# Routed results of a second MoE layer: written tile by tile and gathered, or scattered to a row per token and expert and loaded plainly

## The chip, the cores and the metric

The kernel runs on one core of one Trainium2 chip. The core has TensorE (PE; its weight loads are listed apart as PEld), VectorE (DVE), ScalarE (ACT), GpSimd (POOL) and SyncE (SP), each with an instruction queue of its own, and 16 DMA engines. In this kernel SP issues the plain DMAs and POOL the indirect ones. The metric is the device time in microseconds of one execution, the median of several runs.

## The reference

Two transformer blocks over 8 sequences of 512 tokens with 256 features, float32. Block 0: causal attention with rotary positions, then a mixture of 32 experts (top 8, inner size 96). Block 1: causal attention with a fused projection, then a mixture of 16 experts (top 2, inner size 176) and a shared expert (inner size 352). The change sits in the last of these:

```python
scores = softmax(t @ gate_w.T)
weights, indices = top_k(scores, 2)            # 2 of 16 experts for each token
for e in range(16):
    w_e = sum(where(indices == e, weights, 0))
    y = y + swiglu(t, w1[e], w3[e], w2[e]) * w_e[:, None]
z = swiglu(t, sw1, sw3, sw2)                   # shared expert
return x + y + z
```

with swiglu(t, a, b, o) = (silu(t a') * (t b')) o'. Each token therefore has two routed results, which are added to its row of x.

## The kernel before

**Routing.** The routed layers don't multiply every token with every expert. While a layer's attention runs, `route` works out for each token and each of its chosen experts a row in a DRAM buffer `xg`, in which every expert has a slab, and POOL scatters the token's normalized row there with indirect DMAs of 128 rows (L385). Behind a row's 256 features stand its weights for the layer's experts, so in layer 1 an `xg` row has 272 floats. The rows behind each slab's last token, up to the next full tile, are overwritten with zeros. `tables` then finds, for a list of tiles of 128 rows, where each begins (`rowi`) and which expert it belongs to (`offi`); the list has a fixed length, so some of its tiles hold few or no tokens.

**Parts.** Layer 1 is split: part 0 holds sequences 0 to 5 (60 tiles), part 1 sequences 6 and 7 (28 tiles).

**Experts.** `experts` goes over the tiles in 44 pairs, in five stages that are spread over the steps s of one loop: `load` of pair s (SP loads two tiles of `xg`, 7 buffers), `turn_x` of pair s-4 (PE transposes, DVE copies to `xgTs`, L1108), `gate_up` of pair s-5 (PE, L1131; ACT silu, L1136; DVE multiplies with the other half and with the row's weight, which it takes from the `xg` row at an offset in a register, L1123), `turn_h` of pair s-6 (PE transposes, DVE copies to `hTs`, L1152) and `down` of pair s-7 (PE `y`, L1162; ACT copies it to `ys`, L1167; SP writes the 256 KB of a pair to consecutive rows of `yg`, L1168). PE's order is the order in which this loop is written; the order of the other engines' instructions is chosen by the scheduler.

**Results.** When part 0 is through, `results` runs beside part 1's pairs. For each sequence, `begin` fetches x back, and `gather_rows` works out which rows of `yg` hold each token's two results (L1186 to L1192 on DVE: two tensor operations, four MAX8, one conversion); POOL gathers them in 8 indirect DMAs of 128 rows into two tiles `g` (L1262). DVE adds both to x (L1274), PE transposes x (`xout`, L1284), ACT copies it (L1285) and SP writes the output (L1286). `begin` of the next sequence is issued before the adds of the current one. `Beside.step` spreads these steps evenly over the loop: 8 steps for each sequence from `done`, the 38th step, to `end`. Sequences 6 and 7 come after the loop, from the second call of `results` in `last_part`, and nothing runs beside them.

A second, general version of the whole computation stands behind a branch (L1516) for inputs that the fast version can't treat; it is not executed with these inputs.

Of the kernel before, what the change touches and what calls it, by code (L numbers as in the profile page):

```python
# [90 lines left out]
def two_blocks_kernel(  # L91
# [117 lines left out]
    class Layer:  # L209
        def __init__(self, n, part, seqs, n_e, k, gu):  # L210
            self.n, self.part, self.seqs, self.n_e, self.k, self.gu = n, part, seqs, n_e, k, gu
            self.name = f"{n}{part}"
            self.w_r = rw[:, : ND * E0] if n == 0 else rw[:, ND * E0 :]

            self.cap = len(seqs) * T + P


            self.most_tiles = len(seqs) * T * k // P + n_e
            self.n_tiles = len(seqs) * T * k // P + n_e // 2 + (6 if n_e > 16 else 4)
            name = self.name  # L220

            self.width = D + n_e
            self.xg = drp.tile([n_e * self.cap + P, self.width], F32, tag=f"xg{name}", name=f"xg{name}")
            self.yg = drp.tile([self.most_tiles * P, D], F32, tag=f"yg{name}", name=f"yg{name}")

            self.slab = cpool.tile([P, n_e], F32, tag=f"slab{name}", name=f"slab{name}")
            nc.gpsimd.iota(
                self.slab, [[self.cap, n_e]], base=1, channel_multiplier=0, allow_small_or_imprecise_dtypes=True
            )
            self.next = cpool.tile([P, n_e], F32, tag=f"next{name}", name=f"next{name}")  # L230
            nc.vector.tensor_copy(self.next, self.slab)
            self.shift = cpool.tile([P, n_e], F32, tag=f"shift{name}", name=f"shift{name}")

            def routes(what, width, dtype):
                return {
                    b: rpool.tile([P, NT, width], dtype, tag=f"{what}{n}", name=f"{what}{n}_{b}") for b in seqs
                }

            self.keys, self.chosen = routes("key", n_e, F32), routes("chosen", n_e, BF16)
# [73 lines left out]
    def ffn_parts(smp, bank):  # L313
        def route(n, b, xn, xT, name, again):
# [65 lines left out]
                nc.vector.max(out=keys[:, t, :], in_=key[:, t, :])  # L380
            rows = rpool.tile([P, NT, k], U32, tag=f"rows{n}", name=f"rows_{name}", bufs=4)
            nc.vector.tensor_scalar(rows, keys[:, :, :k], -1.0, 0.0, ALU.add, ALU.max)  # L382
            for t in range(NT):
                for i in range(k):
                    inst = nc.gpsimd.indirect_dma_start(  # L385
                        out=lay.xg, out_offset=bass.IndirectOffsetOnAxis(ap=rows[:, t, i : i + 1], axis=0),
                        in_=xn[:, t, :], in_offset=None,
                    )
                    tc.declare_no_dep(inst.ins, group=group, reason="no two tokens have the same row")
                    tc.add_to_no_dep_group(group, inst.ins)  # L390
# [671 lines left out]
    def experts(n, gu, dn, mp, ps, again, beside):  # L1062
# [48 lines left out]
        def gate_up(lay, i):  # L1111
            part = lay.part
            xT, xg = made.pop(("xT", part, i)), made.pop(("xg", part, i))
            h = mp.tile([P, 2, inner], F32, tag="h", name=f"h_{name}_{part}_{i}")
            if n == 0:
                whole = ps.tile([P, 2, 2 * inner], F32, tag="gu", name=f"gu_{name}_{part}_{i}")
                gus = [whole[:, 0, :], whole[:, 1, :]]
            else:
                gus = [ps.tile([P, 2 * inner], F32, tag="gu", name=f"gu_{name}_{part}_{i + j}") for j in range(2)]

            def scaled(j):

                nc.vector.scalar_tensor_tensor(  # L1123
                    h[:, j, :], h[:, j, :], xg[:, j, D:][:, bass.ds(offs[part, i + j][2], 1)], gus[j][:, inner:],
                    ALU.mult, ALU.mult,
                )

            for j in range(2):
                at = offs[part, i + j][0]
                for c in range(ND):  # L1130
                    nc.tensor.matmul(  # L1131
                        gus[j], xT[:, j, c, :], gu[:, bass.ds(at + c * 2 * inner, 2 * inner)],
                        start=(c == 0), stop=(c == ND - 1),
                    )
                if n:
                    nc.scalar.activation(h[:, j, :], gus[j][:, :inner], AF.Silu)  # L1136
                    scaled(j)
            if n == 0:
                nc.scalar.activation(h, whole[:, :, :inner], AF.Silu)  # L1139
                for j in range(2):  # L1140
                    scaled(j)
            made["h", part, i] = h
# [12 lines left out]
        def down(lay, i):  # L1155
            part = lay.part
            hT = made.pop(("hT", part, i))
            y = ps.tile([P, 2, D], F32, tag="y", name=f"y_{name}_{part}_{i}")
            for j in range(2):
                at = offs[part, i + j][1]  # L1160
                for q, (lo, n_in) in enumerate(chunks):
                    nc.tensor.matmul(  # L1162
                        y[:, j, :], hT[:n_in, q, j, :], dn[:n_in, bass.ds(at + q * D, D)],
                        start=(q == 0), stop=(q == n_ch - 1),
                    )
            ys = mp.tile([P, 2, D], F32, tag="ys", name=f"ys_{name}_{part}_{i}", bufs=4)
            nc.scalar.copy(ys, y)  # L1167
            nc.sync.dma_start(out=lay.yg[i * P : (i + 2) * P, :].rearrange("(j p) d -> p j d", p=P), in_=ys)  # L1168

# [6 lines left out]
                beside.step(s)  # L1178
            beside.finish()

    def gather_rows(n, b, gat, again=""):

        lay = lay_of(n, b)
        n_e, k, name = lay.n_e, lay.k, f"{n}{again}_{b}"
        key = gat.tile([P, NT, n_e], F32, tag="ykey", name=f"ykey{name}", bufs=1)
        nc.vector.tensor_tensor(key, lay.keys[b], lay.shift.unsqueeze(1).to_broadcast([P, NT, n_e]), ALU.add)  # L1186
        nc.vector.tensor_tensor(key, key, lay.chosen[b], ALU.mult)
        keys = gat.tile([P, NT, 8], F32, tag="ykeys", name=f"ykeys{name}", bufs=2)
        for t in range(NT):
            nc.vector.max(out=keys[:, t, :], in_=key[:, t, :])  # L1190
        rows = rpool.tile([P, NT, k], U32, tag=f"yrows{n}", name=f"yrows{name}")
        nc.vector.tensor_scalar(rows, keys[:, :, :k], -1.0, lay.tiles(bool(again)) * P - 1.0, ALU.add, ALU.min)  # L1192
        for i in range(k):
            for t in range(NT):
                yield i, t, lay.yg[: lay.tiles(bool(again)) * P, :], bass.IndirectOffsetOnAxis(ap=rows[:, t, i : i + 1], axis=0)

    def gathers(n, b, gat, again=""):

        for i, t, yg, rows in gather_rows(n, b, gat, again):
            nc.gpsimd.indirect_dma_start(  # L1200
                out=xs[b][:, t, :], out_offset=None, in_=yg, in_offset=rows, compute_op=ALU.add
            )
            if t % 2:
                yield

    def load_attn(pool, src, cols, width, layer):
        t = pool.tile([P, width], F32, tag="attn_w", name=f"attn_w{layer}")
# [47 lines left out]
    def results(seqs, gat, op, ps, again="", behind=lambda: None):  # L1255


        def begin(b):
            fetch_x(b, x_after[1], f"c1{again}")
            made[b] = [gat.tile([P, NT, D], F32, tag="gath", name=f"g1{again}_{b}_{i}", bufs=2 * K1) for i in range(K1)]  # L1260
            for i, t, yg, rows in gather_rows(1, b, gat, again):
                nc.gpsimd.indirect_dma_start(out=made[b][i][:, t, :], out_offset=None, in_=yg, in_offset=rows)  # L1262
                if t % 2:
                    yield

        made = {}
        yield from begin(seqs[0])
# [54 lines left out]
    def all_experts(n, gw, gat, again=False, weights=()):  # L1322
# [6 lines left out]
        with ExitStack() as s:  # L1329
# [11 lines left out]
            def x_in_ring():  # L1341
                for b in range(SPLIT[0]):
                    fetch_x(b, x_after[0], f"a1{g}")
                yield
                for b in range(SPLIT[0]):
                    yield from gathers(0, b, gat, g)

            def x_kept():
                with tc.issue_after(beside.load):
# [19 lines left out]
            if n == 0:  # L1369
                beside.add(done, end, SPLIT[0] * 16 + 1, x_in_ring())  # L1370
            else:
                beside.add(
                    done, end, SPLIT[1] * 8, results(range(SPLIT[1]), gat, gat, ps, g, lambda: beside.last)
                )
            experts(n, gw, dw, mp, ps, again, beside)
            return beside.last
# [28 lines left out]
    with ExitStack() as s1:  # L1405
# [4 lines left out]
        with ExitStack() as s:  # L1410
# [7 lines left out]
            def ahead1(b):  # L1418
                if b >= SPLIT[0]:
# [1 line left out]
                    with tc.issue_after(fetched):  # L1421
                        load_gate_up(gw1, f1, I1, N1R, b - SPLIT[0], NB - SPLIT[0])
                    yield
                    yield from gathers(0, b, gat)

            def after1(b):
                name = f"f1_{b}"
                xn = layernorm(xs[b], lnp, name, "xn_rows", 1, E1)
                yield from free()
                xT = yield from turned(xn, lnp, bank, name)  # L1430
                yield from route(1, b, xn, xT, name, False)
# [43 lines left out]
    def general1(gat):  # L1475
        with ExitStack() as s:
# [20 lines left out]
            def all_of(b, name):  # L1497
                if b >= SPLIT[0]:
                    fetch_x(b, x_after[0], "a1g")
                    drain(gathers(0, b, gat, "g"))  # L1500
                yield from attention1(b, w)
                xn = layernorm(xs[b], lnp, name, "xn_rows", 1, E1)
                xT = yield from turned(xn, lnp, bank, name)
                yield from route(1, b, xn, xT, name, True)
                yield from shared(sw1, xT, xs[b], name)
# [179 lines left out]
```

## Time and profile before

| | us |
|---|---|
| median of 3 runs | 1705.48 |
| lowest, highest | 1697.82, 1710.20 |
| profiled execution | 1701.29 |
| its span in the trace | 1699.6 |
| first gate-and-up product of layer 1's experts | 1428.71 |
| first gather of part 0's results | 1590.09 |
| last y of the experts ends | 1663.48 |
| last add to x begins | 1688.68 |

The profile is one execution; the span is what the trace covers of it, and the mean granted TensorE clock in it was 0.961 of full speed. Durations of single instructions come from that execution. In a list of instructions, "[0.30 <-issue]" gives the idle time of the engine before the instruction and what ended it. In a table of stretches, each engine has its busy time and, in brackets, its number of instructions.

### The profile page before, as it was taken

The numbers are of one execution on the slowest core, as the hardware profiler recorded it, in microseconds if no ns is written. First come the engines' busy times: TensorE is split into PE (matmuls) and PEld (weight loads), VectorE is DVE, ScalarE is ACT, GpSimd is POOL, SyncE is SP. The second block draws the span as 40 slices with busy tenths as digits, with TensorE's granted clock in tenths as the row PEclk, the third lists the DMA queues.
The fourth block names the chain that finished last, engine by engine and source line by source line (L and its number), as shares of the span: only waits on it lengthen the run. The fifth ranks groups of instructions, "written<-read, shape, count | busy, mean of one in ns | idle before, by whom it ended". The sixth has DMA issues, their size and how long they took to land. (4 is left out here: it accounts for less than half of the span.)

```text
span 1699.6 us, 30922 instructions
## 1 busy us (share of the span) xinstructions
PE 1543.7 (91%) x10180; PEld 1029.0 (61%) x10180; DVE 992.0 (58%) x3131; ACT 650.7 (38%) x865; POOL 792.1 (47%) x660
## 2 busy tenths in 40 slices
PE   5899999995999999999989999999899988999982
PEld 2455454543898999998853454544444545777761
DVE  5678887875555555555455764764656544444452
ACT  2555554552233333333334554454355331222221
POOL 0017677577710004888888448888511011000473
PEclk9999999997999999999999999999899998999996
DMA  2035557236988778999995245664312024343563
GB/s 73 13 87 156 163 167 270 102 139 207 307 256 269 202 201 226 266 264 273 268 194 71 39 107 80 127 136 72 86 52 79 26 84 159 109 159 116 156 225 120
DMA packets 255128, 259.43 MB, mean 153 GB/s; under 512 B 80212, under 2 KB 235988, under 8 KB 254964
## 3 DMA queue, kind: packets, MB, share of 16 engines
q1 hardware_dynamic: 199172, 167.88, 32.5%
q0 software_dynamic: 55296, 88.65, 23.0%
q8 instruction: 87, 1.43, 0.4%
q10 hardware_dynamic: 496, 0.85, 0.1%
q14 instruction: 77, 0.63, 0.1%
HBM read 132.70 MB, written 124.57 MB: 151 GB/s over the span
## 5 line engine op out<-in xcount | busy, mean ns | idle before, releaser
L1200 POOL DMA_INDIRECT x_a<-yg,yrows x256 | 402.9, 1574 | 277.2 <-DMA xg_m<-xg 181.9
L385 POOL DMA_INDIRECT xg<-xn_f,rows_f x320 | 321.2, 1004 | 414.7 <-DVE rows_f L382 197.3
L643 ACT ACTIVATE p_a<-st_a 128x2048 f32<-128x2048 f32 (+1 forms) x192 | 306.1, 1594 | 276.4 <-PE st_a L638 243.2
L1131 PE MATMUL gu_m<-gw,xgTs_m 128*128 x1552 | 335.6, 360 | 4.9 <-DVE xgTs_m L1108 3.0
L1131 PEld LDWEIGHTS gu_m<-gw,xgTs_m 128*128 128x128 f32 x1552 | 258.1, 192 | 33.9 <-DVE xgTs_m L1108 3.2
L1162 PE MATMUL y_m<-dw,hTs_m 96*128 (+1 forms) x952 | 237.7, 379 | 0.0
L638 PE MATMUL st_a<-qT_a,kT_a 32*128 32x512 f32 (+3 forms) x2048 | 202.1, 478 | 11.1 <-ACT p_a L643 10.8
L649 DVE TENSOR_TENSOR p_a<-p_a,causal 128x512 f32<-128x512 f32 x256 | 170.8, 686 | 57.3 <-ACT p_a L643 56.1
L661 PE MATMUL o_a<-p_a,v 128*32 128x512 f32 (+3 forms) x2048 | 197.4, 455 | 6.9 <-DVE p_a L649 6.7
L1108 DVE COPY xgTs_m<-xgT_m 128x512 f32<-128x512 f32 x194 | 133.9, 690 | 109.7 <-PE xgT_m L1106 109.4
L1167 ACT COPY ys_m<-y_m 128x512 f32<-128x512 f32 x194 | 113.7, 586 | 189.1 <-PE y_m L1162 174.7
L1123 DVE SCALAR_TENSOR_TENSOR h_m<-h_m,xg_m,gu_m 128x96 f32<-128x96 f32 (+1 forms) x388 | 114.8, 326 | 115.2 <-ACT h_m L1136 69.3
L1162 PEld LDWEIGHTS y_m<-dw,hTs_m 96*128 96x128 f32 (+1 forms) x952 | 165.3, 190 | 15.1
L1262 POOL DMA_INDIRECT g<-yg,yrows x64 | 65.2, 1018 | 202.2 <-DVE h_m L1123 170.9
L638 PEld LDWEIGHTS st_a<-qT_a,kT_a 32*128 32x128 f32 x2048 | 90.1, 189 | 107.2 <-issue 52.4
L1152 DVE COPY hTs_m<-hT_m 96x256 f32<-96x256 f32 (+1 forms) x194 | 92.7, 478 | 99.5 <-PE hT_m L1151 98.5
L1106 PE MATMUL xgT_m<-ident,xg_m 128*128 128x128 f32 x776 | 119.3, 275 | 16.0 <-DMA xg_m<-xg 13.2
L1139 ACT ACTIVATE h_m<-gu_m 128x192 f32<-128x192 f32 x150 | 49.7, 331 | 212.2 <-PE gu_m L1131 200.6
L1106 PEld LDWEIGHTS xgT_m<-ident,xg_m 128*128 128x128 f32 x776 | 95.6, 141 | 39.2 <-issue 16.6
L661 PEld LDWEIGHTS o_a<-p_a,v 128*32 128x32 f32 x2048 | 49.3, 110 | 107.8 <-issue 66.1
L1151 PE MATMUL hT_m<-ident,h_m 128*96 128x128 f32 (+1 forms) x476 | 84.9, 274 | 0.6 <-DVE h_m L1123 0.4
L667 DVE COPY osb_a<-o_a 128x512 f32<-128x512 f32 x64 | 44.0, 688 | 53.0 <-PE o_a L661 53.0
(198 smaller groups left out, 1689.6 us busy)
## 6 DMA issues: line engine op xcount, KB each, us to landing
yg<-ys_m SPq DMA_DIRECT2D x194, 256.0 KB
xg_m<-xg SPq DMA_DIRECT2D x300, 144.0 KB
xg_m<-xg SPq DMA_DIRECT2D x88, 136.0 KB
xg<-zeros SPq DMA_DIRECT2D x66, 144.0 KB
xg<-xn_f,rows_f POOLq DMA_INDIRECT x320
xg<-zeros SPq DMA_DIRECT2D x34, 136.0 KB
xf<-in_x_dram SPq DMA_DIRECT2D x8, 512.0 KB
x_after<-x_in SPq DMA_DIRECT2D x8, 512.0 KB
```

Source lines behind the costliest of these rows:

```text
L385: inst = nc.gpsimd.indirect_dma_start(out=lay.xg, out_offset=bass.IndirectOffsetOnAxis(ap=rows[:, t, i : i + 1], axis=0), in_=xn[:, t, :], ...
L638: nc.tensor.matmul(st[:, g, at : at + T - j * P], kT[r, j * P : (j + 1) * P], qT[r, j * P :], start=True, stop=True,)
L643: nc.scalar.activation(pt, st[:, :, :width], AF.Exp, scale=SCALE)
L649: self.masked = nc.vector.tensor_tensor(d, d, causal.unsqueeze(1).to_broadcast([P, NG, P]), ALU.mult).ins
L661: nc.tensor.matmul(o[32 * g : 32 * g + 32, j * P :], v1[:, j, v_at + g * (DH + 1) :][:, :32], probs[n][:, g, at : at + T - j * P], start=( ...
L1106: nc.tensor.transpose(tr[:, j, c, :], xg[:, j, c * P : (c + 1) * P], ident)
L1108: nc.vector.tensor_copy(xT, tr)
L1123: nc.vector.scalar_tensor_tensor(h[:, j, :], h[:, j, :], xg[:, j, D:][:, bass.ds(offs[part, i + j][2], 1)], gus[j][:, inner:], ALU.mult, A ...
L1131: nc.tensor.matmul(gus[j], xT[:, j, c, :], gu[:, bass.ds(at + c * 2 * inner, 2 * inner)], start=(c == 0), stop=(c == ND - 1),)
L1162: nc.tensor.matmul(y[:, j, :], hT[:n_in, q, j, :], dn[:n_in, bass.ds(at + q * D, D)], start=(q == 0), stop=(q == n_ch - 1),)
L1167: nc.scalar.copy(ys, y)
L1200: nc.gpsimd.indirect_dma_start(out=xs[b][:, t, :], out_offset=None, in_=yg, in_offset=rows, compute_op=ALU.add)
```

## The change

In layer 1 each routed row also carries where its result belongs. Layer 0 keeps its way.

- An `xg` row of layer 1 has 288 floats instead of 272: behind the 16 weights stand 16 integers. For a token that an expert was chosen for, the integer is the number of the token's result row plus one: the token's place in the part for its expert with the higher row, and the same plus the number of the part's tokens for the other. `route` writes them with two more DVE operations for each sequence; the token numbers come from an iota on POOL at the start. Rows of zeros carry 0.
- `gate_up` takes, for each of a pair's two tiles, the integer of the tile's expert minus one into a column of `to` (one DVE operation of 128x1 each; the tile has 5 buffers).
- `down` doesn't write `ys` with SP. POOL scatters it with two indirect DMAs of 128 rows of 1 KB, at the row numbers in `to`; a number out of bounds (the -1 of empty rows) is skipped.
- `yg` of layer 1 is thus ordered by token. `begin` loads a sequence's two tiles `g` with two plain DMAs of 512 KB on SP; the work of `gather_rows` and the gathers are gone from layer 1, and `gather_rows` is merged into layer 0's `gathers`.
- `results` beside part 1 begins two steps later and has 6 steps for each sequence.

```diff
-            self.width = D + n_e
+            self.width = D + n_e * (1 + n)
...
+                self.yg = drp.tile([k * len(seqs) * T, D], F32, tag=f"yg{name}", name=f"yg{name}")
+                self.tokens = cpool.tile([P, len(seqs), NT], F32, tag=f"tokens{name}", name=f"tokens{name}")
+                nc.gpsimd.iota(
+                    self.tokens, [[T, len(seqs)], [1, NT]], base=1, channel_multiplier=NT,
+                    allow_small_or_imprecise_dtypes=True,
+                )
...
             nc.vector.tensor_scalar(rows, keys[:, :, :k], -1.0, 0.0, ALU.add, ALU.max)
+            if n:
+                nc.vector.tensor_tensor(key, key, keys[:, :, 0:1].to_broadcast([P, NT, n_e]), ALU.is_lt)
+                tokens = lay.tokens[:, b - lay.seqs[0], :].unsqueeze(2).to_broadcast([P, NT, n_e])
+                nc.vector.scalar_tensor_tensor(
+                    xn[:, :, D + n_e :].bitcast(I32), key, float(len(lay.seqs) * T), tokens, ALU.mult, ALU.add
+                )
...
             h = mp.tile([P, 2, inner], F32, tag="h", name=f"h_{name}_{part}_{i}")
+            if n:
+                to = made["to", part, i] = mp.tile([P, 2], I32, tag="to", name=f"to_{name}_{part}_{i}", bufs=5)
+                for j in range(2):
+                    nc.vector.tensor_scalar(
+                        to[:, j : j + 1], xg.bitcast(I32)[:, j, D + lay.n_e :][:, bass.ds(offs[part, i + j][2], 1)],
+                        -1.0, None, ALU.add,
+                    )
...
             nc.scalar.copy(ys, y)
-            nc.sync.dma_start(out=lay.yg[i * P : (i + 2) * P, :].rearrange("(j p) d -> p j d", p=P), in_=ys)
+            if n == 0:
+                nc.sync.dma_start(out=lay.yg[i * P : (i + 2) * P, :].rearrange("(j p) d -> p j d", p=P), in_=ys)
+                return
+            to = made.pop(("to", part, i))
+            for j in range(2):
+                inst = nc.gpsimd.indirect_dma_start(
+                    out=lay.yg, out_offset=bass.IndirectOffsetOnAxis(ap=to.bitcast(U32)[:, j : j + 1], axis=0),
+                    in_=ys[:, j, :], in_offset=None, bounds_check=lay.k * len(lay.seqs) * T - 1, oob_is_err=False,
+                )
...
             made[b] = [gat.tile([P, NT, D], F32, tag="gath", name=f"g1{again}_{b}_{i}", bufs=2 * K1) for i in range(K1)]
-            for i, t, yg, rows in gather_rows(1, b, gat, again):
-                nc.gpsimd.indirect_dma_start(out=made[b][i][:, t, :], out_offset=None, in_=yg, in_offset=rows)
-                if t % 2:
-                    yield
+            for i in range(K1):
+                lo = (i * len(lay.seqs) + b - lay.seqs[0]) * T
+                nc.sync.dma_start(out=made[b][i], in_=lay.yg[lo : lo + T, :].rearrange("(p t) d -> p t d", t=NT))
+                yield
...
-                    done, end, SPLIT[1] * 8, results(range(SPLIT[1]), gat, gat, ps, g, lambda: beside.last)
+                    done + 2, end, SPLIT[1] * 6, results(range(SPLIT[1]), gat, gat, ps, g, lambda: beside.last)
...
-                xn = layernorm(xs[b], lnp, name, "xn_rows", 1, E1)
+                xn = layernorm(xs[b], lnp, name, "xn_rows", 1, 2 * E1)
```

More of the change, by code (lines that the diff above doesn't have):

```diff
@@ L220, in __init__ @@
             name = self.name
-            self.width = D + n_e
+            self.width = D + n_e * (1 + n)
             self.xg = drp.tile([n_e * self.cap + P, self.width], F32, tag=f"xg{name}", name=f"xg{name}")
-            self.yg = drp.tile([self.most_tiles * P, D], F32, tag=f"yg{name}", name=f"yg{name}")
+            if n == 0:
+                self.yg = drp.tile([self.most_tiles * P, D], F32, tag=f"yg{name}", name=f"yg{name}")
+            else:
+                self.yg = drp.tile([k * len(seqs) * T, D], F32, tag=f"yg{name}", name=f"yg{name}")
[4 more added lines that the diff above has]
+                )
             self.slab = cpool.tile([P, n_e], F32, tag=f"slab{name}", name=f"slab{name}")
@@ L1167, in down @@
             nc.scalar.copy(ys, y)
-            nc.sync.dma_start(out=lay.yg[i * P : (i + 2) * P, :].rearrange("(j p) d -> p j d", p=P), in_=ys)
+            if n == 0:
+                nc.sync.dma_start(out=lay.yg[i * P : (i + 2) * P, :].rearrange("(j p) d -> p j d", p=P), in_=ys)
[6 more added lines that the diff above has]
+                )
+                tc.declare_no_dep(inst.ins, group=f"to_{name}_{part}", reason="each token's row is one expert's")
+                tc.add_to_no_dep_group(f"to_{name}_{part}", inst.ins)
         stages = [(load, 0), (turn_x, 4), (gate_up, 5), (turn_h, 6), (down, 7)]
@@ L1179, in experts, with gathers @@
             beside.finish()
-    def gather_rows(n, b, gat, again=""):
-        lay = lay_of(n, b)
-        n_e, k, name = lay.n_e, lay.k, f"{n}{again}_{b}"
+    def gathers(b, gat, again=""):
+        lay = lay_of(0, b)
+        n_e, k, name = lay.n_e, lay.k, f"{again}_{b}"
         key = gat.tile([P, NT, n_e], F32, tag="ykey", name=f"ykey{name}", bufs=1)
@@ L1190, in gather_rows @@
             nc.vector.max(out=keys[:, t, :], in_=key[:, t, :])
-        rows = rpool.tile([P, NT, k], U32, tag=f"yrows{n}", name=f"yrows{name}")
+        rows = rpool.tile([P, NT, k], U32, tag="yrows", name=f"yrows{name}")
         nc.vector.tensor_scalar(rows, keys[:, :, :k], -1.0, lay.tiles(bool(again)) * P - 1.0, ALU.add, ALU.min)
@@ L1194, in gather_rows @@
             for t in range(NT):
[L1195 to L1202, printed above, removed]
-            if t % 2:
-                yield
+                nc.gpsimd.indirect_dma_start(
+                    out=xs[b][:, t, :], out_offset=None, in_=lay.yg[: lay.tiles(bool(again)) * P, :],
+                    in_offset=bass.IndirectOffsetOnAxis(ap=rows[:, t, i : i + 1], axis=0), compute_op=ALU.add,
+                )
+                if t % 2:
+                    yield
     def load_attn(pool, src, cols, width, layer):
@@ L1259, in begin @@
             fetch_x(b, x_after[1], f"c1{again}")
+            lay = lay_of(1, b)
             made[b] = [gat.tile([P, NT, D], F32, tag="gath", name=f"g1{again}_{b}_{i}", bufs=2 * K1) for i in range(K1)]
-            for i, t, yg, rows in gather_rows(1, b, gat, again):
-                nc.gpsimd.indirect_dma_start(out=made[b][i][:, t, :], out_offset=None, in_=yg, in_offset=rows)
-                if t % 2:
-                    yield
+            for i in range(K1):
+                lo = (i * len(lay.seqs) + b - lay.seqs[0]) * T
+                nc.sync.dma_start(out=made[b][i], in_=lay.yg[lo : lo + T, :].rearrange("(p t) d -> p t d", t=NT))
+                yield
         made = {}
@@ L1345, in x_in_ring @@
                 for b in range(SPLIT[0]):
-                    yield from gathers(0, b, gat, g)
+                    yield from gathers(b, gat, g)
             def x_kept():
@@ L1423, in ahead1 @@
                     yield
-                    yield from gathers(0, b, gat)
+                    yield from gathers(b, gat)
             def after1(b):
                 name = f"f1_{b}"
-                xn = layernorm(xs[b], lnp, name, "xn_rows", 1, E1)
+                xn = layernorm(xs[b], lnp, name, "xn_rows", 1, 2 * E1)
                 yield from free()
@@ L1499, in all_of @@
                     fetch_x(b, x_after[0], "a1g")
-                    drain(gathers(0, b, gat, "g"))
+                    drain(gathers(b, gat, "g"))
                 yield from attention1(b, w)
-                xn = layernorm(xs[b], lnp, name, "xn_rows", 1, E1)
+                xn = layernorm(xs[b], lnp, name, "xn_rows", 1, 2 * E1)
                 xT = yield from turned(xn, lnp, bank, name)
```

## The prediction

> **What bounds the kernel now.** I read the page's busy shares first, then a table of 20 us stretches of the last 300 us, then the order of time inside one of them, then the chain that ended last. The shares say TensorE:
>
> ```profile
> PE 1543.7 (91%) x10180; PEld 1029.0 (61%) x10180; DVE 992.0 (58%) x3131; ACT 650.7 (38%) x865; POOL 792.1 (47%) x660
> ```
>
> The change sits in the second layer, so a share over the whole span says little. The stretches (length, then busy time of PE, PEld, DVE, ACT and POOL, granted clock, DMA share, GB/s):
>
> ```profile
> 1560.00:1580.00 20.00, 20.00 (x98) 15.28 (x98) 8.44 (x17) 4.88 (x12) 0.00 (x0) 1.00 0.35 110
> ...
> 1600.00:1620.00 20.00, 17.59 (x87) 12.95 (x86) 11.19 (x21) 5.32 (x12) 15.60 (x15) 1.00 0.72 224
> ...
> 1680.00:1700.00 20.00, 2.77 (x11) 1.59 (x9) 2.77 (x4) 2.15 (x4) 5.28 (x6) 0.50 0.32 103
> ```
>
> Three regimes: in the experts PE is busy 20.00 of 20 us (DVE 8.44, POOL idle); once part 0's results are fetched beside part 1's tiles PE loses some 2 us in 20; in the last 36 us almost nothing runs but POOL's gathers. The chain of the last 36 us (start, length, what):
>
> ```profile
> 1663.52 0.59 ACT ys_m L1167
> ...
> 1664.13 2.12 DMA yg<-ys_m
> ...
> 1667.06 2.81 DMA g<-yg,yrows
> ...
> 1685.80 2.76 DMA g<-yg,yrows
> ...
> 1688.68 0.70 DVE x_c L1274
> ```
>
> A pair of tiles takes 4.97 us in the steady stage; one such iteration by its order of time:
>
> ```profile
> 1569.33 1.89 PE L1162 MATMUL y_m<-dw,hTs_m 88*128 x8
> ...
> 1571.30 0.59 ACT L1167 COPY ys_m<-y_m 128x512 f32<-128x512 f32 x1 [1.89 <-PE y_m L1162]
> ...
> 1571.69 0.69 DVE L1108 COPY xgTs_m<-xgT_m 128x512 f32<-128x512 f32 x1 [1.26 <-PE xgT_m L1106]
> ...
> 1573.23 0.40 DVE L1123 SCALAR_TENSOR_TENSOR h_m<-h_m,xg_m,gu_m 128x176 f32<-128x176 f32 x1 [0.84 <-ACT h_m L1136]
> ...
> 1576.47 2.53 PE L1131 MATMUL gu_m<-gw,xgTs_m 128*128 x8
> ```
>
> DVE copies xgTs some 4 us before the next gate-and-up product (1576.47) needs it: that slack is what the new wait is weighed against.
>
> **1. The tail, removed and added.** Before: after the last y (1661.59 + 1.89 = 1663.48) come the copy, the 256 KB write (landed 1666.24), 16 gathers 1.25 us apart (0.95 + 0.30 each) from 1667.06, and the last add ends 1689.37, 25.9 us after y. After: the copy ends 1664.11; two scatters. Their nearest rows are the route's scatters, same engine, 128 rows each:
>
> ```profile
> 1217.59 0.96 POOL L385 DMA_INDIRECT xg<-xn_f,rows_f  x1 [0.30 <-issue]
> 1220.13 1.38 DVE L292 TENSOR_SCALAR xn_f<-x_a,mv_f,rstd_f 128x256 f32<-128x256 f32 x4 [5.36 <-DMA xg<-xn_f,rows_f]
> ```
>
> So 0.96 + 0.30 each, and 2.54 us from a scatter's start until DVE, which waited for its landing, runs. POOL starts 0.27 us after its releaser (rows_f ends 1409.38, scatter 1409.65). Hence 1664.11 + 0.27 = 1664.38; second scatter 1665.64; landed 1668.18. Then four loads of 512 KB: the load of x_c issued at 1195.25 let DVE read at 1198.60, 3.35 us, so the first is in at 1671.5. For each further one, 0.524 MB at the 406 to 417 GB/s that the best slices of this window reach is 1.3 us; with the outputs written beside them I take 1.6: 1676.3. Two adds of 0.69: 1677.7. That is 14.2 us after y, **-11.6**. Ends: -12.7 with 1.3 us each; -6.4 if each load took 3.35 alone.
>
> **2. The new wait, the cost that speaks against the change.** The `to` tile has 5 buffers, so the `to` of pair j may be written only once both scatters of pair j-5 have landed, and it is VectorE that waits. Nearly all `to` wait for scatters two iterations back, which is free by some 4 us. But in VectorE's order as built, eight of them (pairs 5, 9, 13, 17, 21 and 27 of part 0, 1 and 5 of part 1, counted from 0) stand one iteration early: ahead of the xgTs copy of the iteration that directly follows the y of pair j-5. Queued behind are xgTs, two h products and hTs, and PE's next gate-and-up waits for xgTs and (its PSUM buffer) the first h. In the iteration shown: y ends 1571.22, copy 1571.89, POOL 1572.16, second scatter 1573.42, landed 1575.96; two `to` 0.3 (small DVE rows: 0.13 to 0.17), xgTs 0.69, h 0.40, and starts between them 0.1: 1577.45, against 1576.47 now. PE stands 0.95 us. 8 x 0.95 = **+7.6**; a ninth (`to` of pair 25, behind xgTs but ahead of h) 0.3.
>
> This is also the most uncertain price: no row shows a scatter that checks bounds and skips rows, nor POOL started by ACT. Each us more from y's end to landing costs eight full us here, about one for the ninth and one in the tail: ten in all. Cheap end: landing 0.95 us earlier, no stall, 0; below that nothing, since a wait on DVE can't speed PE. Dear end: POOL starting 0.82 late as the first gather did (1666.24 to 1667.06), scatters of 1.54 (the accumulating form at L1200) and landing in 3.67 (the slowest gather of the chain, issued at 1682.06): 0.55 + 0.58 + 1.13 = 2.3 us, +23. I take the scatter rows, as engine, direction and size are theirs.
>
> The Trainium skill, "DMA: Bandwidth & Descriptors", section "Anatomy of one DMA — SWDGE (gpsimd) path", gives a POOL DMA about 2.0 us fixed plus bytes over 436e3, most of it the receipt of the write, and calls main memory the heaviest target: this speaks against waiting for scatters inside the loop. Its figure for 128 KB, 2.3 us, an estimate, would make the stall 0.7 if counted from the scatter's start, and 1.7 (+13.4) if counted after the 0.96 us of issuing. The rows' 2.54 from the start lies between and is what I use.
>
> **3. Adds and outputs.** PE waits at each sequence's output:
>
> ```profile
> PE xout L1284 <- DVE x_c L1274: 6.0, 7, 1.2
> ```
>
> Results now begin two iterations later and take 6 steps instead of 8; in the built order sequences 0, 2 and 3 get their adds an iteration ahead of their transposes. Three waits of 1.1 to 1.2 go: **-3.5** (0 to -4). The adds keep their 2.48 us on DVE.
>
> **4. Start of the experts.** xgT is turned at 1426.15 but xgTs is copied at 1427.97, because the row numbers of three sequences (2.4 us of `ykey` rows) stand ahead; these go. In their place come a register load (0.35 to 2.05 us on DVE's sequencer, median 0.85) and two `to` (0.4): **-0.8** (-1.8 to +0.5).
>
> **5. Route.** Two more DVE operations of 128x64 per sequence (rows L377 and L335: 0.22), eight times: 3.7 us of DVE in an attention stage where it is the second engine. Sequence 7's pair hides in DVE's 3.08 us wait for su_f at 1409.4 to 1412.45. **+1.5** (0 to 3.7).
>
> **At nothing:** 44 writes on SP (nobody waits but the tail) and 48 of 64 gathers, which ran beside PE-bound work; the xg rows of 144 instead of 136 KB, fetched with 7 buffers, over two iterations early, at a DMA share of 0.35 to 0.53; 2 x 1.26 us of POOL in a 4.97 us iteration where it is idle; 88 `to` of about 0.2 us, DVE being busy 8.44 of 20. SP: sequence 0's load waits for part 0's last scatter ahead of an xg load, which has two iterations to spare. Without that cover one iteration would lose up to 2.5 us, a scatter's landing.
>
> **Sum:** -11.6 + 7.6 + 0.3 - 3.5 - 0.8 + 1.5 = -6.5. Profiled run 1701.3 - 6.5 = 1694.8; median 1705.5 - 6.5 = 1699.0, the profiled run lying 4.2 below it. **Forecast 1697.** About 1% (17 us) is what a measurement of this kernel can tell from no change.
>
> **Rivals.**
> - *Late scatters (slower than before).* The landing in step 2 comes 1 to 3 us later than the row: +10 to +30, 1707 to 1727. For it: bounds and skipped rows are unseen, and the wait is on VectorE ahead of everything PE needs. Against: 320 route scatters average 1004 ns and eight gathers beside this very loop 951. Below +0.65 us it is still a gain; from +2.5 us it is slower by over 1%. 0.2, in most of it beyond 1%.
> - *The wait is free.* The scatter lands a us sooner, many rows being skipped (part 1 has 16 tiles' worth of rows in 28 tiles): -6.5 - 7.9 = -14.4, 1687 to 1691. 0.2.
> - *It does little of what it says.* The gain is only at the tail, and there four loads serialize behind outputs: -6.4 instead of -11.6, about 1702. 0.1.
> - Forecast, 1691 to 1702: 0.5.
>
> The range reaches into both sides: 1683 (free wait, best tail) to 1716 (landing 2 us late). Faster by over 1% 0.2, within 0.62, slower 0.18.
>
> **What would show it.** Steady stretches without early `to` keep PE at 20.00 of 20; every fourth iteration has a gap of about 1 us ahead of gu, released by DVE, with DVE idle before a `to` on the yg scatter. Scatter rows of about 0.96 us; last y to last add 14 us; PE waits for x_c near 2.5 us in all. I am wrong if the scatters cost 1.5 us or more, if DVE's waits last longer than 4.5 us, or if the loads at the end come in one by one.

## The result, and the profile after

The changed kernel takes 1704.95 us (median of 12 runs, 1700.85 to 1709.96), the kernel before, run beside it, 1703.13 us (12 runs): a ratio of 1.0002, 95% interval 0.9987 to 1.0018. No difference that can be measured. The profiled execution of the changed kernel took 1707.52 us, span 1705.8.

That nothing moved is the sum of large moves that cancel. The table cuts both profiled executions at the same instructions: the first transposed tile of layer 1's experts, ACT's copies of y (one for each pair, 0 to 43), the end of the last add to x. Each length is the difference of two instants in the order of time.

| stretch | before, us | after, us | difference |
|---|---|---|---|
| start to the first turned tile | 1425.49 | 1428.15 | +2.66 |
| first turned tile to the copy of pair 0 | 15.52 | 12.32 | -3.20 |
| copy of pair 0 to pair 31 | 155.16 | 162.31 | +7.15 |
| copy of pair 31 to pair 43 | 67.35 | 77.85 | +10.50 |
| copy of pair 43 to the end of the last add | 25.85 | 14.66 | -11.19 |
| from there to the end of the span | 10.23 | 10.51 | +0.28 |

The first row can't be put down to the change: in the nine profiled kernels of this study that have the change, which are alike there, it lies between 1421.6 and 1434.0 us, while the second and third rows come out the same to 0.01 us wherever the order of instructions agrees. From the first turned tile on, the change costs 3.54 us in the profile.

The busy shares hardly move (POOL, which has 88 scatters for 64 gathers, most):

```profile
PE 1551.6 (91%) x10180; PEld 1034.3 (61%) x10180; DVE 995.5 (58%) x3179; ACT 650.1 (38%) x865; POOL 822.4 (48%) x686
```

In the stretches of 20 us of the changed kernel (the columns are those of before) PE is no longer full in the steady stage, and falls to 15.70 where part 0's results are loaded, at a granted clock of 0.83:

```profile
1560.00:1580.00 20.00, 19.40 (x94) 14.56 (x93) 8.98 (x24) 4.76 (x12) 7.70 (x8) 1.00 0.34 105
...
1600.00:1620.00 20.00, 15.70 (x68) 11.51 (x67) 6.85 (x19) 3.34 (x8) 4.87 (x5) 0.83 0.56 189
...
1640.00:1660.00 20.00, 17.15 (x74) 12.44 (x73) 8.11 (x20) 4.91 (x11) 6.39 (x6) 0.85 0.67 237
...
1680.00:1700.00 20.00, 4.92 (x23) 3.69 (x21) 5.17 (x8) 3.81 (x7) 3.47 (x4) 0.58 0.45 164
```

**A steady stall**, in the order of time of the changed kernel. The scatter issued at 1505.55 releases the `to` at 1508.08, 2.53 us later; xgTs, h and gu follow, and PE has stood 0.59 us:

```profile
1505.55 0.98 POOL L1197 DMA_INDIRECT yg<-ys_m,to_m  x1 [0.30 <-issue]
...
1508.08 0.29 DVE L1135 TENSOR_SCALAR to_m<-xg_m 128x1 int32 x2 [3.96 <-DMA yg<-ys_m,to_m]
1508.28 0.68 DVE L1124 COPY xgTs_m<-xgT_m 128x512 f32<-128x512 f32 x1
1508.88 0.70 DVE L1147 SCALAR_TENSOR_TENSOR h_m<-h_m,xg_m,gu_m 128x176 f32<-128x176 f32 x2
...
1509.33 0.56 PE L1155 MATMUL gu_m<-gw,xgTs_m 128*128 x1 [0.59 <-DVE h_m L1147]
```

**The same wait where the results are loaded.** Four plain loads of 512 KB start at 1599.00 to 1601.9; the scatter issued at 1599.95 among them releases its `to` only at 1606.15, 6.20 us later, and PE stands 4.30 us:

```profile
1599.00 0.33 SPq L1294 DMA_DIRECT2D g<-yg  x1
...
1599.95 0.98 POOL L1197 DMA_INDIRECT yg<-ys_m,to_m  x1 [0.30 <-issue]
...
1600.48 1.41 SPq L1294 DMA_DIRECT2D g<-yg  x3
...
1606.15 0.28 DVE L1135 TENSOR_SCALAR to_m<-xg_m 128x1 int32 x2 [6.80 <-DMA yg<-ys_m,to_m]
...
1607.44 0.95 PE L1155 MATMUL gu_m<-gw,xgTs_m 128*128 x1 [4.30 <-DVE h_m L1147]
```

**The outputs**, 45 us on. The write of an output issued at 1647.75, beside result loads and fetches of x, holds the only tile `xo` until 1654.7; ACT's next copy of `xout` waits 2.46 us for it, PE's transposes 2.85 us for ACT, and the eight products gu after it take 4.22 us instead of 2.53:

```profile
1647.75 0.38 SPq L1317 DMA_DIRECT2D out_dram<-xo  x1
...
1654.78 1.07 ACT L1316 COPY xo<-xout 128x512 f32<-128x512 f32 x2 [2.46 <-DMA out_dram<-xo]
...
1655.42 0.66 PE L1122 MATMUL xgT_m<-ident,xg_m 128*128 128x128 f32 x4 [2.85 <-ACT xo L1316]
...
1655.91 4.22 PE L1155 MATMUL gu_m<-gw,xgTs_m 128*128 x8
```

Between these two places, at 1638.96, PE stood 2.25 us for a late add. VectorE had waited at a `to` first, then worked off the products and the copy behind it, and only then came to the adds:

```profile
1635.75 0.29 DVE L1135 TENSOR_SCALAR to_m<-xg_m 128x1 int32 x2 [1.61 <-DMA yg<-ys_m,to_m]
...
1636.93 2.48 DVE L1305 TENSOR_TENSOR x_c<-x_c,g 128x512 f32<-128x512 f32 x4
...
1638.96 1.20 PE L1315 MATMUL xout<-ident,x_c 128*128 128x128 f32 x4 [2.25 <-DVE x_c L1305]
```

**The clock behind the stops.** With each of these three stops of PE (they end at 1607.44, 1638.96 and 1655.42) came a stretch in which the granted clock was 0.50, half of full speed (the column before the DMA share). From 1440 to 1604 us it is 1.00:

```profile
1604.90:1611.60 6.70, 4.16 (x7) 2.52 (x8) 3.13 (x8) 0.32 (x1) 0.98 (x1) 0.50 0.63 239
...
1639.00:1642.30 3.30, 3.30 (x11) 2.54 (x12) 1.11 (x2) 0.58 (x1) 2.26 (x2) 0.50 0.83 245
1656.10:1659.40 3.30, 3.30 (x7) 1.80 (x7) 2.25 (x6) 0.32 (x1) 0.00 (x0) 0.50 0.73 295
```

In the first, the eight products gu take 4.71 us instead of 2.53. A stop there costs its length and the slow products after it.

**The tail**: last scatter, four loads, adds, the last copy.

```profile
1683.40 0.98 POOL L1197 DMA_INDIRECT yg<-ys_m,to_m  x1 [0.30 <-issue]
1686.20 1.75 SPq L1294 DMA_DIRECT2D g<-yg  x4
1690.03 5.26 DVE L1305 TENSOR_TENSOR x_c<-x_c,g 128x512 f32<-128x512 f32 x8 [11.66 <-DMA g<-yg]
...
1698.07 1.07 ACT L1316 COPY xo<-xout 128x512 f32<-128x512 f32 x2 [3.18 <-DMA out_dram<-xo]
```

The waits of 1600 to 1681 us in the changed kernel (engine, line, releaser: us in total, times, longest):

```profile
DVE to_m L1135 <- DMA yg<-ys_m,to_m: 23.3, 6, 7.1
...
PE gu_m L1155 <- DVE h_m L1147: 5.1, 2, 4.3
...
PE xout L1315 <- DVE x_c L1305: 3.4, 2, 2.3
...
ACT xo L1316 <- DMA out_dram<-xo: 2.5, 1, 2.5
```

### The profile page after: what moved, and what is told of

Same layout as the page of the kernel before. It is cut to its first block, busy times and chain, and to the rows that moved or that the text cites. A ratio compares the mean times of both kernels' runs of the same rounds, so it can differ in the third digit from the quotient of the medians.

```text
span 1705.8 us, 31140 instructions
## 1 busy us (share of the span) xinstructions
PE 1551.6 (91%) x10180; PEld 1034.3 (61%) x10180; DVE 995.5 (58%) x3179; ACT 650.1 (38%) x865; POOL 822.4 (48%) x686
## 4 chain that ended last, share of the span: by engine, by line
PE 47%; POOL 19%; issue 14%; DVE 10%; DMA 5%; ACT 2%; SPq 2%; POOLq 0%; DVEq 0%; ACTq 0%
POOL x_a L1229 15%; PE gu_m L1155 7%; PE st_a L654 7%; PE o_a L677 6%; PE y_m L1186 4%; PE qkv_a L859 3%; PE xgT_m L1122 2%; POOL yg L1197 2%; PE sg_f L418 2%; POOL xg L401 2%; ACT p_a L659 2%; DVE p_a L665 2%; PE y_a L743 2%; PE su_f L418 2%; PE sy_f L431 2%
## 5 line engine op out<-in xcount | busy, mean ns | idle before, releaser
L1155 PE MATMUL gu_m<-gw,xgTs_m 128*128 x1552 | 339.1, 362 | 13.2 <-DVE h_m L1147 10.1
L654 PE MATMUL st_a<-qT_a,kT_a 32*128 32x512 f32 (+3 forms) x2048 | 200.9, 476 | 11.2 <-ACT p_a L659 11.0
L1197 POOL DMA_INDIRECT yg<-ys_m,to_m x88 | 94.0, 1068 | 167.8 <-ACT ys_m L1191 153.2
```

The costliest lines, as they stand in the source:

```text
L654: nc.tensor.matmul(st[:, g, at : at + T - j * P], kT[r, j * P : (j + 1) * P], qT[r, j * P :], start=True, stop=True,)
L1155: nc.tensor.matmul(gus[j], xT[:, j, c, :], gu[:, bass.ds(at + c * 2 * inner, 2 * inner)], start=(c == 0), stop=(c == ND - 1),)
L1197: inst = nc.gpsimd.indirect_dma_start(out=lay.yg, out_offset=bass.IndirectOffsetOnAxis(ap=to.bitcast(U32)[:, j : j + 1], axis=0), in_=ys[: ...
```

## The experiments

Two theories for the changed kernel's loop. **A**: VectorE stands at a `to` that the built order puts too early, for scatters that were only just issued; beside the big loads these land late. **B**: behind pair 31 it is the results' own pace (their loads, adds and outputs) that costs, and the wait at `to` only shows it. Ratios are to the kernel before, run on the same chip, with 95% intervals.

### 1. The `to` pinned late (late8)

```diff
-            nc.vector.tensor_copy(xT, tr)
+            made["turned", part, i] = nc.vector.tensor_copy(xT, tr).ins
...
-                to = made["to", part, i] = mp.tile([P, 2], I32, ..., bufs=5)
+                to = made["to", part, i] = mp.tile([P, 2], I32, ..., bufs=8)
                 for j in range(2):
+                    with tc.issue_after(made["turned", part, i]):
                         nc.vector.tensor_scalar(to[:, j : j + 1], ...)
```

> The `to` operations are pinned behind the xgTs copy of their own pair and have 8 buffers, so that each waits for scatters eight pairs back; nothing else changes. Theory A (the loss in the loop is VectorE standing at an early `to`): the steady stretches return to PE 20.00 of 20, ACT's copy of pair 31 comes 7 us earlier, the 11.6 us iteration of pair 32 shrinks to about 5, and the kernel takes 12 to 17 us less than the change, about 0.991 of before. Theory B (the loss behind pair 31 is the pace of the results, their loads and outputs, and the wait at `to` only shows it): only the 7 us of the steady part go, the last 12 pairs still take some 77 us, and the kernel is at 0.996 of before.

Measured: 1684.61 us, ratio 0.9882 (0.9848 to 0.9916). No `to` waits for a scatter any more. Pairs 0 to 31 take 155.15 us, to 0.01 us the time of before; pair 32 takes 4.97; the last 12 pairs take 63.39 us. PE is full again in its stretches (pinned kernel):

```profile
1560.00:1580.00 20.00, 20.00 (x98) 15.30 (x97) 9.20 (x25) 4.88 (x12) 7.87 (x8) 1.00 0.34 106
1600.00:1620.00 20.00, 20.00 (x98) 15.30 (x97) 11.15 (x30) 4.88 (x12) 8.32 (x8) 1.00 0.67 215
```

Theory A holds, for the last 12 pairs too: with the same loads, adds, outputs and pace they take 14.46 us less. Pair by pair these are 6.65 at pair 32, 1.07 at 36, 2.49 at 37 and 4.25 at 39, and nothing elsewhere. Part of this is the clock, which now stays up for the whole loop (pinned kernel):

```profile
1420.00:1668.00 248.00, 240.74 (x1159) 180.08 (x1157) 118.22 (x314) 60.92 (x146) 98.38 (x95) 1.00 0.46 151
```

By how much longer PE's instructions took in the three slow stretches of the changed kernel (2.2 us at pair 32, 1.8 at 37, 1.7 at 39), I estimate the clock's part at some 5.7 of the 14.46 us. No run takes it away without the stops. The gain of 20 us on the changed kernel is above the 12 to 17 expected: 7.16 + 14.46 = 21.6 in the trace.

### 2. The same place with 5 buffers (late5)

The edit of experiment 1 with `bufs=5`.

> The `to` operations pinned behind their own pair's xgTs copy, with the 5 buffers of the change: place alone, without more buffers. If the place decides: steady iterations of 4.97 us throughout, and the last 12 pairs within 2 us of the 63.4 us that the pinned kernel with 8 buffers took (a `to` then waits for scatters issued one and a half iterations, some 6 us, before it, and the longest landing seen was 6.2). If the buffers were needed too: several iterations of the last 12 pairs stay 1 to 3 us long.

Measured: 1683.38 us, ratio 0.987 (0.984 to 0.990). Pairs 0 to 31 155.16 us, the last 12 pairs 63.40. VectorE still waits three times for a scatter behind 1600 us, 3.3 us in all and at most 1.4, and none of it reaches PE. At the pinned place five buffers do as well as eight.

### 3. More buffers alone (to10)

`bufs=10` for `to` in the changed kernel, nothing else.

> The only edit is 10 buffers for `to` instead of 5. In the built order every `to` moves some four iterations ahead with it, so that nine of them still stand one iteration early. Theory A: a `to` still waits for scatters that were just issued, steady stalls of about 0.9 us at every fourth pair stay, time within 0.3% of the change. Rival (too few buffers is the cause as such): the stalls are gone and 12 us or more with them.

Measured: 1690.64 us, ratio 0.9924 (0.9904 to 0.9944). My expectation failed: the steady stalls are gone (155.15 us). As I read the built order, every `to` moved some four iterations ahead for five more buffers, so that each won one iteration, about 5 us, on its scatters, more than their 2.5. What VectorE met in exchange is the load that a `to` reads from (waits of 1440 to 1600 us):

```profile
DVE to_m L1135 <- DMA xg_m<-xg: 28.0, 28, 5.2
```

That is hidden but for one place: pair 32, where the xg load stands beside the result loads, takes 8.88 us, 3.9 too long: PE stands 2.20 us, and its granted clock is 0.50 for the next 3 us. The last 12 pairs take 67.36.

### 4. Smaller result loads (small)

```diff
-                nc.sync.dma_start(out=made[b][i], in_=lay.yg[lo : lo + T, :].rearrange("(p t) d -> p t d", t=NT))
+                nc.sync.dma_start(out=made[b][i][:, :1, :], in_=lay.yg[lo : lo + T, :].rearrange("(p t) d -> p t d", t=NT)[:, :1, :])
...
-                            xs[b][:, lo : lo + 2, :], xs[b][:, lo : lo + 2, :], g[:, lo : lo + 2, :], ALU.add
+                            xs[b][:, lo : lo + 2, :], xs[b][:, lo : lo + 2, :], g[:, 0:1, :].to_broadcast([P, 2, D]), ALU.add
```

> Leaves out three quarters of the result loads: each plain load brings 128 KB instead of 512 KB, and the adds use these rows for all four (same instructions, same sizes on VectorE). Theory that the loads stretch the scatters: the wait at the `to` before pair 32 falls from 6.8 us to 3 or less, and that iteration from 11.6 us to about 6. Rival (POOL or VectorE slow the scatters): that iteration stays above 9 us.

Measured: 1698.02 us in its one run. With the early `to` left as it was, pair 32 takes 6.64 us instead of 11.62. Its scatter lands after 3.30 us instead of 6.20 (small-load kernel):

```profile
1599.83 0.98 POOL L1197 DMA_INDIRECT yg<-ys_m,to_m  x1 [0.30 <-issue]
1603.13 0.28 DVE L1135 TENSOR_SCALAR to_m<-xg_m 128x1 int32 x2 [4.96 <-DMA yg<-ys_m,to_m]
```

The wait itself fell to 4.96 us, not to 3 as expected, since it begins earlier; the iteration is as expected. It is the size of the loads that stretches the scatter: POOL's part of it, 0.98 us, is the same in both. The last 12 pairs take 70.21 us, so that the load size explains 7.6 of the 14.5 us, net of one pair that got worse: pair 37 takes 11.39 us instead of 9.54, because PE stands 3.27 us there for a late add and then has 0.50 of its clock again. Smaller loads alone don't cure the late adds.

### 5. Earlier results (sched, late8sched)

```diff
-                    done + 2, end, SPLIT[1] * 6, results(...)
+                    done, end, SPLIT[1] * 6, results(...)
```

On the changed kernel:

> Only the pace of the results is put back to the earlier start (two steps earlier), still 6 steps for each sequence. Theory A: the steady part is as in the change (pair 31 within 1 us); the last 12 pairs change by less than 5 us either way, since the loads still come four at a time. Theory B (the later start crowds loads and outputs): the last 12 pairs take 7 us or more less than the 77.9 us of the change.

Measured: 1696.81 us, ratio 0.9971 (0.9951 to 0.9992). The steady part is unchanged (162.05 us), pair 32 takes 12.16, but the last 12 pairs take 69.06, 8.8 less than in the change, which is what theory B said. On the pinned kernel:

> Pinned, 8 buffers, and results begin two steps earlier, still 6 steps for each sequence. With the wait in place that earlier start took 8.8 us from the last 12 pairs. If the pace only mattered through the wait: last 12 pairs at 62 to 65 us, time as the pinned kernel within 0.2%. If the pace costs by itself: 58 to 61 us.

Measured: 1680.89 us, ratio 0.9861 (0.9832 to 0.9889), last 12 pairs 60.33 us, 3.1 less than pinned alone. So B has a share: the later start costs 3.1 us by itself, and 8.8 us together with the wait. With the earlier start the wait still costs 7.2 us at pair 32, but only some 1.6 us in the pairs behind it, where it was 7.8: those 7.8 need both, the waits at `to` and the later start. That they come from late adds, which bunch the outputs behind the one tile `xo`, is how I read the rows of 1635 to 1656 us; no run takes it alone.

### 6. Two output tiles (late8xf2, late8both)

`bufs=2` for `xo` in the pinned kernel.

> Pinned, 8 buffers, and two output tiles xo instead of one. The pinned kernel's last ACT copy waited 3.79 us for the write of sequence 6's output. Expected: that wait is gone and the end comes 2 to 3.5 us earlier after the last y, 0.998 of the pinned kernel; the loop itself unchanged (63 us for the last 12 pairs). Rival: the last two writes then only queue behind one another and nothing is won.

Measured: 1680.42 us, ratio 0.9863 (0.9833 to 0.9893). From the last add to the end 8.57 us instead of 10.28. The wait for the output write is gone from the last copy (two-tile kernel), which in the pinned kernel had been 3.79 us:

```profile
1668.02 1.07 ACT L1316 COPY xo<-xout 128x512 f32<-128x512 f32 x2 [2.07 <-PE xout L1315]
```

A gain of 1.7 us in the trace, below the 2 to 3.5 expected: the copy now waits 2.07 us for PE's transposes, and only the difference to 3.79 is won. The last version has all three edits:

> Pinned `to` with 8 buffers, results begin two steps earlier, two output tiles xo. If the two gains lie in different places (the loop's last 12 pairs: 60.3 us instead of 63.4; after the last add: 8.6 us instead of 10.3), they add: some 5 us below the pinned kernel, 0.984 to 0.986 of before. If the earlier start only shifts work into the tail, 0.987 or more.

Measured: 1680.81 us, ratio 0.9868 (0.9844 to 0.9893). In the trace the gains add (60.41 us for the last 12 pairs, 8.71 after the last add), in the times they don't show: with the stage ahead differing by several us from run to run, the pinned versions, all between 0.986 and 0.988, can't be told apart. Each of them beats both kernels.

### 7. The route's part alone (carry)

The kernel before with rows of 288 floats, the iota and the two operations for each sequence:

```diff
+            if n:
+                second = smp.tile([P, NT, n_e], F32, tag="second", name=f"second_{name}")
+                nc.vector.tensor_tensor(second, key, keys[:, :, 0:1].to_broadcast([P, NT, n_e]), ALU.is_lt)
+                tokens = lay.tokens[:, b - lay.seqs[0], :].unsqueeze(2).to_broadcast([P, NT, n_e])
+                nc.vector.scalar_tensor_tensor(
+                    xn[:, :, D + n_e :].bitcast(I32), second, float(len(lay.seqs) * T), tokens, ALU.mult, ALU.add
+                )
```

> The kernel before with one part of the change alone: rows of 288 floats in layer 1, the iota, and two more VectorE operations for each sequence that write the row numbers (onto a scratch tile); nobody reads them, results are written and gathered as before. Expected from the prediction's step 5: +1.5 us (0 to 3.7), ratio 1.000 to 1.002. Rival that the added route work or the wider rows cost more than that: 1.004 or more.

Measured: 1703.10 us, ratio 0.9997 (0.9983 to 1.0011). No cost that can be seen; more than 1.9 us is excluded. In its trace only the start of the experts differs from before (first turned tile to pair 0's copy 16.86 us instead of 15.52), and that is the clock: PE stands 1.85 us ahead of the first product in both, and the half clock that comes with it lasts 6.8 us here and 3.4 us before.

## Why the prediction was right, and where a step was not

The time lies in the range and within 1% of before, which had 0.62, but 8 us above the forecast, between the case of 1691 to 1702 and the 1707 at which *late scatters* began. The mechanism of the new wait was right, the size of the loop's loss was not: 4.4 us were forecast for it (7.6 + 0.3 - 3.5), and 17.65 came. That the sum still ended so near to before is in part luck: 2.4 us came back at the start of the experts, 1.4 of them a slow stretch of the clock in the kernel before that the prediction knew nothing of. The prediction's steps, against the stretches of the table:

1. **The tail.** Forecast -11.6, measured -11.19. The last add ends 14.7 us after the last y (14.2). The parts: the last scatter starts 0.7 us later than worked out, because an earlier one took 3.76 us beside the adds; it lands in 2.75 (2.54); the first load is in after 3.83 us (3.35); the other three come in faster than 1.6 us each.
2. **The wait of VectorE.** The mechanism, its places and in the steady stage its size were right. POOL starts 0.27 us after ACT, a scatter takes 0.98 (0.96) where no add runs beside it, and lands in 2.46 to 2.53 (2.54). The early `to` of pairs 5, 9, 17 and 27 cost 0.84 to 0.87 us each, that of pair 13 0.56 (0.95 forecast); pair 21's cost 1.65, because its scatter, beside SP's writes of zeros, landed in 3.28. Pair 25's cost 0.64 (0.3). With pair 31's 0.87 that makes the +7.15 of pairs 0 to 31, where seven times 0.95 and 0.3 give 6.95. **The step that failed is the eighth**: priced at 0.95 like the others, it cost 6.65. I had the sensitivity, one us of stall for each us of landing, and left it at one landing for all places, although the change itself puts 2 MB of plain loads where this one falls. 6.20 - 2.54 = 3.7 us of it are the landing; with the usual 0.6 PE stood 4.30, and 2.2 us are the gu products after it, at a granted clock of 0.50, for which the prediction had no term. Experiment 1 shows it gone without the wait, experiment 4 shrunk with the loads. The sign that I gave for being wrong here, a wait of VectorE of more than 4.5 us, came true and was a poor one: ahead of the early `to` of the steady stage VectorE waited 3.5 to 5.8 us at a cost of 0.56 to 1.65, ahead of the eighth 6.80 at a cost of 6.65. What costs is when the scatter lands, not how long VectorE has been standing. (The terms written down for one stall give 1577.45 - 1576.47 = 0.98, not 0.95.)
3. **Adds and outputs.** Forecast -3.5, and the last 12 pairs should have taken 67.35 - 3.5 + 0.95 = 64.8 us; they took 77.85. Without the wait they take 63.39 (experiment 1), -3.96: the step itself was right. What I left out is that later `to` stand ahead of the adds on VectorE: late adds make late transposes (2.25 us at 1638.96), two outputs then come close together, and the second waits for the first to leave the only `xo`. It comes to 7.8 us at pairs 36, 37 and 39, some 3.5 of them at the half clock behind the two stops. I had called these `to` free.
4. **Start of the experts.** Forecast -0.8, measured -3.20. To the first gate-and-up product it is 3.22 us before and 1.44 after, -1.78, my lower bound; the register load that I put in its place hid. (The terms that I gave, 1.8 us gone against 0.85 and 0.4 us new, make -0.6, not -0.8.) The other 1.4 us are the clock again, which I hadn't counted. Before, PE stands 1.85 us ahead of that product, and the first of the eight products run at a granted clock of 0.50; after, it stands 0.31 us, and they run at 1.00. From the first product to the copy of pair 0 it is 12.30 us before and 10.88 after. The first row is of the kernel before, the second of the changed one:

```profile
1428.20:1431.60 3.40, 2.89 (x5) 1.85 (x6) 2.25 (x14) 0.14 (x1) 0.00 (x0) 0.50 0.02 5
...
1429.00:1432.00 3.00, 2.93 (x12) 1.86 (x12) 2.49 (x14) 0.32 (x1) 0.00 (x0) 1.00 0.00 0
```

5. **Route.** Forecast +1.5, measured -0.5 with an interval of -2.9 to +1.9: not resolved, the upper half of the bounds excluded.

The sum without the route was forecast at -8.0 and is +3.5 in the trace. The difference of 11.5 us is step 2's eighth `to` (+5.7) and step 3's chain (+7.8, less the 0.5 that its own gain was larger), with +0.4 from the tail, +0.2 from the other `to` and +0.3 after the last add, less the 2.4 us of step 4.

Of the rivals, *late scatters* named what happened and its sign, but as one delay for all places; it happened at one of them and in the chain behind it. *The wait is free* fell: every early `to` cost 0.56 us or more. The rival that the gain is little of what it says fell: the tail kept 11.2 of 11.6 us.

On the delay, the Trainium skill bears in "DMA: Bandwidth & Descriptors", section "Issuing engines are not separate DMA queues": transfers issued by different engines run on the same 16 DMA engines and interleave. The rows agree: POOL's 128 KB land in 2.46 to 2.53 us in the steady stage, 3.28 beside writes of zeros, 3.30 beside four loads of 128 KB, 6.20 beside four of 512 KB.

## What to carry to other kernels

A buffer's reuse is a wait that the program doesn't show: look in the built order at which engine takes it and what stands behind it there, since the scheduler moved this cheap operation ahead as its buffers let it. Pinning it behind the work that it belongs to was worth 20 us here, and more buffers alone less. And a landing time read in one stage isn't the landing time beside the transfers that the change itself adds; a wait that is priced at half a microsecond or so is to be priced at the worst place, not at the typical one. There it can also bring the half clock, which a sum of waits doesn't hold.

## What the hardware showed that I had not expected

- A scatter's issue on POOL, 0.98 us, took up to 3.76 us beside VectorE's adds of two SBUF tiles (changed kernel), more than the 2.09 us of a gather beside them before:

```profile
1675.47 3.76 POOL L1197 DMA_INDIRECT yg<-ys_m,to_m  x1 [0.30 <-issue]
...
1675.88 2.48 DVE L1305 TENSOR_TENSOR x_c<-x_c,g 128x512 f32<-128x512 f32 x4
```

  It ended 0.87 us after the adds. The Trainium skill, "SBUF — State Buffer", section "SBUF: two separate sides", says that a VectorE operation with two SBUF inputs and a GpSimd operation that reads SBUF take a shared pair of ports exclusively, and that the one that starts later waits. These rows agree only in part. The scatter's row ends only behind the adds, and beside VectorE's copies from PSUM the scatters keep their 0.98. But by its row the scatter began 0.41 us ahead of the adds, and it was the scatter that got longer, not they; and in the tail of before, gathers that lie beside 0.5 to 0.7 us of an add take 0.94 to 1.00 us, hardly more than others.
- A short stop of PE costs more than its length. In the 11 traces, between the first turned tile of layer 1's experts and their last y, every stop of PE of 1.85 us or more came with a stretch at half the granted clock, and none of the 25 stops of 1.07 to 1.40 us did; between 1.40 and 1.85 no row tells. The stretches:

| kernel | stop ends at, us | stop, us | granted clock 0.50 from, us | for, us |
|---|---|---|---|---|
| carry | 1429.1 | 1.85 | 1427.9 | 6.8 |
| before | 1428.7 | 1.85 | 1428.2 | 3.4 |
| to10 | 1601.7 | 2.20 | 1601.3 | 3.4 |
| changed | 1639.0 | 2.25 | 1639.0 | 3.4 |
| changed | 1655.4 | 2.85 | 1656.0 | 3.4 |
| small | 1633.8 | 3.27 | 1632.1 | 6.8 |
| changed | 1607.4 | 4.30 | 1604.8 | 6.8 |
| sched | 1604.3 | 4.56 | 1602.3 | 6.8 |

  The eight gu products behind the three stops of the changed kernel took 4.71, 3.32 and 4.22 us instead of 2.53.
- From the first turned tile on, profiled executions whose order of instructions agrees repeat to 0.01 us over 31 pairs, while the stage ahead of it varies by 12 us in kernels that are alike there. Cutting the trace at the same instructions resolves what the medians of 4 to 12 runs can't.
